# Multi-query attention block: order of the upper scores, the values and their stores

## Chip, cores and metric

The kernel runs on one core of a Trainium2 chip. A core has five engines with queues of their own: PE (TensorE, matrix products), DVE (VectorE), ACT (ScalarE), POOL (GpSimd) and SP, which here only issues DMA transfers. Each engine works through its queue in order, and they wait for each other by semaphores. The metric is the device time of one execution in microseconds (us).

## What is computed

Sixty-four batches of 128 tokens with 512 features. Each is normalized, sixteen query heads of 64 features share one key and one value head, a null key and value stand ahead of the tokens, a bias for each head is added, a causal mask (which lets each token see the null place, the tokens up to itself) and a mask of absent tokens apply, and the output projection is normalized and added to the input.

```
xn  = layernorm(x) * g_in
q   = (xn @ Wq) as 16 heads of 64, times 64**-0.5
k, v = halves of xn @ Wkv, with the null key and value ahead
sim = q k^T + bias ; causal and token masks -> -max
out = softmax(sim) v ; out = out @ Wo
y   = x + layernorm(out) * g_out
```

All is in float32.

## The kernel before

The order of the instructions is written by hand; tiles with a fixed number of buffers make the waits. Batches are in groups of four (GB = 4). A main loop runs over steps n; step n projects queries for a group ahead, computes keys and values of batch n + 6, scores of batch n + 2, exponentials of batch n + 1 and the weighted values of batch n. Steps up to 57 (P_LAST + 2, with P_LAST = 55) are step_a for even n and step_b for odd n; they form the output projection of two batches with seven half-size products (out_product). Steps 58 to 63 are last_step, which has no query projection left and forms the output projection directly (out_mm).

Scores come in two halves: a "lower" one, the queries of the first 64 tokens against 64 keys (tile lo or the first half of ps), and an "upper" one, the last 64 tokens against 128 keys (tile ps, two PSUM banks, one buffer). Rows for both lie in one SBUF tile S (s in the profile), already filled with bias and mask by POOL (bias_add, L514). The score products (L547) land in PSUM, DVE adds them into S (scores_add: L563 for the split lower home, L565 otherwise) and takes the negative row maximum (scores_max, L570); ACT takes exponentials with the row sums (exps, L579), DVE the reciprocal of the sums (rinv, L596), POOL scales (scale, L600). DVE then transposes S in 32x32 blocks into sb, which has one buffer (blocks_T, L615); in the next step PE multiplies sb with the values vr into four PSUM tiles po (values, L644), and ACT moves them with the null value added into oT (values_out, L661), from which the output projection reads.

region(n) stands at the end of each step and issues: scores of n + 2, lower and upper; the lower add and maximum; values and values_out of batch n; blocks_T of batch n + 1; the upper add of n + 2. The upper maximum follows early in the next step (max_hi). lower_home gives the lower scores two half tiles: in the early steps one in the pool ps_y (tag Y, which is also the home of the normalized output yn, L782 to L788), in steps after 57 one in ps_q (tag a, which the values use too), and always one in ps_w (tag w, two buffers, which the values use too).

Keys and values: kv_mm (L343) gives both for a batch, kv_out (L358) puts them into kvt, a tile of a whole group with one buffer. After the fourth batch of a group, at the end of the step, keys_T transposes the keys into kb (L386), stores them to memory as kd (to_tokens, three DMAs, L367) and loads them back in four copies as kT (L395); values_spread then stores the values as vd (again L367) and loads them in four copies as vr (L378). All of these DMAs are issued by SP, in order, with the batch loads (L122), residual loads (L129) and stores of results (L817).

In the last steps, last_step(n) issues the output product of batch n - 1 (out_mm), then region(n). In step 61 only half of that product is issued ahead of region, the other half in step 62, likewise there.

## Time and profile before

| | |
|---|---|
| median of 3 runs | 1093.63 us (1092.07 to 1096.82) |
| profiled execution, its own time | 1091.44 us |
| its span, first to last instruction | 1089.7 us |
| PE busy | 1059.1 us (97%) |
| PE weight loads | 885.2 us (81%) |
| DVE busy | 769.1 us (71%) |
| ACT busy | 704.3 us (65%) |
| POOL busy | 703.3 us (65%) |
| mean granted TensorE clock | 0.998 |

How to read what follows. A row of the order of time has the start, the duration, the engine, the line, the operation, output and inputs, shapes and count; in square brackets stands the idle time of the engine just before it and what ended it. A row of the waits says who waited for whom, the total in us, how often, and the longest. The chain of waits is followed back from the last instruction to whatever released it. A group row has line, engine, operation, shapes and count, then busy us and mean ns, then idle time before.

### The profile page before, as it was taken

What the parts mean: (1) busy time and instruction counts of PE and PEld (TensorE: products, weight loads), DVE (VectorE), ACT (ScalarE), POOL (GpSimd) and SP (SyncE); (2) the same over time, 40 slices, a digit from 0 to 9 for tenths busy, and PEclk for the clock granted to TensorE, in tenths of its full rate; (3) what the DMA queues carried; (4) which work ended last, traced back from release to release, by engine and by line L of the source; (5) the groups of instructions that cost most, each with busy time, mean ns of one, the idle gap of its engine ahead of it and who ended that gap; (6) DMA issues with size and microseconds to landing.
All of it is one profiled execution on the core that took longest, in us unless ns stands there. A gap on an engine that the chain in (4) does not pass through costs nothing.

```text
span 1089.7 us, 31299 instructions
## 1 busy us (share of the span) xinstructions
PE 1059.1 (97%) x12292; PEld 885.2 (81%) x12292; DVE 769.1 (71%) x1576; ACT 704.3 (65%) x2826; POOL 703.3 (65%) x520
## 2 busy tenths in 40 slices
PE   8989999999999999999999999999999999999887
PEld 7776887888888888888888888888888888888443
DVE  4767677776777777777777777777777777666772
ACT  3446676675676676676676767667667676656672
POOL 3656767576675767667576676758667576756562
PEclk9999999999999999999999999999999999999999
DMA  6413413423134331423424133341413333111211
GB/s 201 140 47 110 142 64 101 137 59 123 62 96 137 89 119 50 134 84 101 137 63 130 64 121 98 101 137 48 139 60 116 114 98 103 58 41 42 74 53 69
DMA packets 69076, 105.14 MB, mean 96 GB/s; under 512 B 9536, under 2 KB 33728, under 8 KB 67136
## 3 DMA queue, kind: packets, MB, share of 16 engines
q1 hardware_dynamic: 68112, 102.08, 30.4%
q8 instruction: 97, 1.59, 0.6%
q10 hardware_dynamic: 816, 1.05, 0.3%
q14 instruction: 51, 0.42, 0.1%
HBM read 67.45 MB, written 35.65 MB: 95 GB/s over the span
## 4 chain that ended last, share of the span: by engine, by line
PE 88%; DVE 4%; DMA 3%; ACT 2%; issue 1%; SPq 1%; POOL 0%; ACTq 0%; DVEq 0%; POOLq 0%
PE pa L476 17%; PE pyX L728 17%; PE pc L476 9%; PE pyY L728 9%; PE po L644 8%; PE pkv L343 5%; PE ps L547 5%; PE pw L476 4%; PE py L675 4%; PE pyw L728 4%; PE lo L547 3%; PE pq L425 1%; ACT s L579 1%; DVE y L788 1%; DMA biasp<-in_fside_16xSxS_dram 1%
## 5 line engine op out<-in xcount | busy, mean ns | idle before, releaser
L579 ACT ACTIVATE s<-s,nmax 128x65 f32<-128x65 f32 (+1 forms) x1024 | 373.2, 373 | 1.4 <-DVE nmax L570 1.4
L600 POOL TENSOR_TENSOR s<-s,rinv 128x512 f32<-128x512 f32 (+1 forms) x128 | 189.5, 1480 | 200.0 <-DVE rinv L596 192.7
L514 POOL TENSOR_TENSOR s<-biasp,mneg 128x1552 f32<-128x1552 f32 x64 | 207.0, 3234 | 68.5 <-DVE sb L615 66.5
L661 ACT ACTIVATE oT<-po,nv 128x256 f32<-128x256 f32 x256 | 100.7, 475 | 158.0 <-PE po L644 157.9
L579 ACT ACTIVATION_READ_ACCUMULATOR s<-s,nmax 128x1 f32 x1024 | 200.1, 195 | 0.0
L728 PE MATMUL pyX<-wT,oT 128*128 128x256 f32 x672 | 161.7, 383 | 0.0
L615 DVE STREAM_TRANSPOSE sb<-s 128x1536 f32<-128x1536 f32 x64 | 113.8, 1778 | 57.1 <-PE po L644 55.0
L728 PEld LDWEIGHTS pyX<-wT,oT 128*128 128x128 f32 x672 | 125.4, 190 | 20.7 <-issue 4.8
L476 PE MATMUL pa<-xS,wq 128*128 128x256 f32 x480 | 123.5, 380 | 1.0 <-ACT ku L487 1.0
L570 DVE TENSOR_REDUCE nmax<-s 128x8 f32<-128x520 f32 (+1 forms) x128 | 122.1, 954 | 2.4
L476 PEld LDWEIGHTS pa<-xS,wq 128*128 128x128 f32 x480 | 90.9, 190 | 14.2 <-ACT ku L487 1.8
L644 PE MATMUL po<-sb,vr 32*64 32x128 f32 (+1 forms) x4096 | 92.4, 306 | 5.8 <-DVE s L563 3.3
L644 PEld LDWEIGHTS po<-sb,vr 32*64 32x64 f32 x4096 | 71.7, 131 | 21.3 <-issue 15.8
L487 ACT COPY ku<-pa 128x256 f32<-128x256 f32 x120 | 44.7, 372 | 64.7 <-PE pa L476 59.5
L565 DVE TENSOR_TENSOR s<-ps,s 128x1024 f32<-128x1024 f32 (+1 forms) x66 | 77.3, 1171 | 2.3 <-PE ps L547 2.3
L708 POOL TENSOR_TENSOR yS<-oT 128x512 f32<-128x512 f32 x28 | 35.7, 1277 | 63.8 <-ACT oT L661 63.8
L563 DVE TENSOR_TENSOR s<-lo,s 128x256 f32<-128x256 f32 x124 | 46.7, 418 | 41.3 <-PE lo L547 41.3
L343 PEld LDWEIGHTS pkv<-wkv,xT 128*128 128x128 f32 x512 | 64.3, 191 | 14.1 <-issue 8.8
L343 PE MATMUL pkv<-wkv,xT 128*128 128x128 f32 x512 | 70.5, 281 | 5.0 <-ACT xT L304 2.5
L547 PE MATMUL ps<-kT,qT 64*64 64x128 f32 (+1 forms) x2112 | 70.0, 268 | 0.0
L291 ACT ACTIVATE x<-x,nmr,rstd 128x512 f32<-128x512 f32 x60 | 48.7, 815 | 27.9 <-DVE nmr L278 25.5
L785 DVE TENSOR_TENSOR yn<-yn,gob 128x512 f32<-128x512 f32 x56 | 39.2, 700 | 38.7 <-ACT yn L782 38.7
(99 smaller groups left out, 2076.9 us busy)
## 6 DMA issues: line engine op xcount, KB each, us to landing
x<-in_x_dram SPq DMA_DIRECT2D x64, 256.0 KB
res<-in_x_dram SPq DMA_DIRECT2D x64, 256.0 KB
out_dram<-y SPq DMA_DIRECT2D x64, 256.0 KB
xd<-xb SPq DMA_DIRECT2D x14, 1024.0 KB
xT<-xd SPq DMA_DIRECT2D x56, 256.0 KB
vr<-vd SPq DMA_DIRECT2D x64, 128.0 KB
kT<-kd SPq DMA_DIRECT2D x64, 64.0 KB
wo<-in_L_cond_Wo_dram SPq DMA_DIRECT2D x1, 2048.0 KB
```

The costliest lines, as they stand in the source:

```text
L343: nc.tensor.matmul(pkv, xT[g][:, t, kc, :], wkv[:, kc, :], start=(kc == 0), stop=(kc == KC - 1),)
L476: nc.tensor.matmul(prod[tag], w[:, kc, f * P : (f + 1) * P], t[:, :, kc, :], start=(start and kc == 0), stop=(kc == HK - 1), skip_group_ch ...
L514: nc.gpsimd.tensor_tensor(S[b], biasp, mneg[:, t].unsqueeze(1).broadcast_to([P, R8, ROW]), ALU.add,)
L547: nc.tensor.matmul(home[r][u * DH : (u + 1) * DH, f, :], qT[g][rows, f, t, hf, u], kT[g][rows, 0 : nk // Q, t, :], start=True, stop=True,)
L565: nc.vector.tensor_tensor(sv, pv, sv, ALU.add)
L570: nc.vector.tensor_reduce(nmax[b][:, hf], S[b][:, :, WITH_NULL[hf]], AX.X, ALU.max, negate=True)
L579: nc.scalar.activation(row, row, AF.Exp, bias=nmax[b][:, hf, k : k + 1], accum_out=rsum[b][:, hf, k : k + 1],)
L600: nc.gpsimd.tensor_tensor(sv, sv, rinvs.pop((b, hf)).unsqueeze(2).broadcast_to([P, R8, sv.shape[2]]), ALU.mult,)
L615: nc.vector.transpose(sb.rearrange("p j e q -> p e j q"), S[b][:, :, 1 : ROW - 1].rearrange("p e (j k) -> p e j k", k=Q),)
L644: nc.tensor.matmul(po[s][rows, to : to + n], vr[g][quad, j, t, :], sb[quad, slots, r * NF : (r + 1) * NF, :], start=(turn == 0), stop=True ...
L661: nc.scalar.activation(oT[b][:, u * NF : (u + 1) * NF, :].rearrange("p f (s q) -> p s f q", q=Q)[:, blocks], po, AF.Identity, bias=nv2,)
L728: nc.tensor.matmul(prod[key], h[:, c, :], w[:, c, :], start=(start and c == 0), stop=(c == HC - 1), skip_group_check=not start,)
```

## The change

The stores of a group's values are issued in kv_out when the group's fourth batch is in, and values_spread only loads them back. In region, the steps up to 57 (early) keep PE's order and add the upper scores ahead of the transpose. The steps after 57 compute the lower scores in the tile of the upper ones, then the values, and the upper scores behind the transpose in the order of issue. In region the values are issued for every step; it is only called from step 0 on.

```diff
+    def to_tokens(out, places):
+        for at, to, n in ((0, 0, 2), (2, 3, 1), (3, 2, 1)):
+            nc.sync.dma_start(
+                out=out[to * Q : (to + n) * Q], in_=places[at * Q : (at + n) * Q]
+            )
+
+    kvts, vds = {}, {}
-    kvts, kvds = {}, {}
 
     def kv_out(m, pkv):
...
             ALU.subtract,
         )
-
-    def to_tokens(out, places):
...
+        if t == GB - 1:
+            vds[g] = dp.tile([P, GB * DH], FP, tag="vd", name=f"vd_{g}")
+            to_tokens(vds[g], kvts[g][:, 1].rearrange("p t d -> p (t d)"))
 
     def values_spread(g):
 
-        vd = dp.tile([P, GB * DH], FP, tag="vd", name=f"vd_{g}")
-        to_tokens(vd, kvts[g][:, 1].rearrange("p t d -> p (t d)"))
+        vd = vds.pop(g)
...
     def lower_home(n):
 
-        pool, tag = (ps_q, "a") if n > P_LAST + 2 else (ps_y, "Y")
         tiles = [
-            pool.tile([P, HE], FP, tag=tag, name=f"lo0_{n}"),
+            ps_y.tile([P, HE], FP, tag="Y", name=f"lo0_{n}"),
             ps_w.tile([P, HE], FP, tag="w", name=f"lo1_{n}"),
         ]
...
     def region(n):
         nb, eb = n + 2, n + 1
+        early = n <= P_LAST + 2
         if nb < B:
-            scores(nb, 0, lower_home(n))
-            scores(nb, 1)
+            scores(nb, 0, lower_home(n) if early else None)
+            if early:
+                scores(nb, 1)
             scores_add(nb, 0)
+        values(n)
+        if nb < B:
             scores_max(nb, 0)
-        if n >= 0:
-            values(n)
-            values_out(n)
+            if early:
+                scores_add(nb, 1)
+        values_out(n)
         if 0 <= eb < B:
             blocks_T(eb)
         if nb < B:
-            scores_add(nb, 1)
+            if not early:
+                scores(nb, 1)
+                scores_add(nb, 1)
             late_max.append(nb)
```

More of the change, by code (lines that the diff above doesn't have):

```diff
@@ L363, in kv_out @@
         )
-    def to_tokens(out, places):
-        for at, to, n in ((0, 0, 2), (2, 3, 1), (3, 2, 1)):
-            nc.sync.dma_start(
-                out=out[to * Q : (to + n) * Q], in_=places[at * Q : (at + n) * Q]
-            )
+        if t == GB - 1:
+            vds[g] = dp.tile([P, GB * DH], FP, tag="vd", name=f"vd_{g}")
+            to_tokens(vds[g], kvts[g][:, 1].rearrange("p t d -> p (t d)"))
     def values_spread(g):
-        vd = dp.tile([P, GB * DH], FP, tag="vd", name=f"vd_{g}")
-        to_tokens(vd, kvts[g][:, 1].rearrange("p t d -> p (t d)"))
+        vd = vds.pop(g)
         vr[g] = hp.tile([P, NQ, GB, DH], FP, tag="vr", name=f"vr_{g}")
```

## The prediction

> **What bounds the kernel now.** I read the chain of waits first, then the busy time by stage and the waits of PE, then the order of time where PE stops.

> ```profile
> span 1089.7 us, 31299 instructions
> ...
> PE 88%; DVE 4%; DMA 3%; ACT 2%; issue 1%; SPq 1%; POOL 0%; ACTq 0%; DVEq 0%; POOLq 0%
> ```

> The span of the profiled execution is 1089.7 us, its time 1091.44 (1.74 around the span), and 88% of the chain that ends last is TensorE. An edit on another engine therefore pays only where PE stops for it.

> ```profile
> 133.00:1009.00 876.00, 869.62 (x10374) 749.41 (x10368) 638.45 (x1334) 590.73 (x2371) 584.23 (x424) 1.00 0.31 95
> 1009.00:1089.70 80.70, 67.72 (x765) 35.29 (x760) 46.49 (x79) 45.68 (x197) 39.71 (x29) 0.97 0.20 65
> ```

> Columns: stretch, its length, busy us of PE, weight loads, DVE, ACT and POOL, granted clock, DMA share, GB/s. From 133 to 1009 us (steps 4 to 57) PE stands still for 6.4 us in 876. In the last 80.7 us (steps 58 to 63 and the end) it is idle for 13.0, and there the clock is below 1. So the early steps and the late steps are two problems.

> PE's waits from 133 to 1009, and where the pair product that opens each even step starts (first, two in the middle, last; the first three from the chain, the fourth from the order of time):

> ```profile
> PE po L644 <- issue: 2.4, 2, 1.9
> PE lo L547 <- DVE y L788: 1.6, 8, 0.2
> PE pkv L343 <- issue: 1.6, 1, 1.6
> ```

> ```profile
> 133.09 1.93 PE pyX L728 x8
> ...
> 622.63 1.92 PE pyX L728 x8
> 654.68 1.92 PE pyX L728 x8
> ```

> ```profile
> 1009.01 1.99 PE L728 MATMUL pyX<-wT,oT 128*128 128x256 f32 x8
> ```

> Two undisturbed steps take 654.68 - 622.63 = 32.05 us. From 133.09 to 1009.01 lie 27 such pairs: 27 x 32.05 = 865.3, but 875.9 passed. That is more than PE's idle time, since the modelled ends of matmuls cover part of a wait. Of the excess of 10.6 us, 4.0 are "issue", waits for nothing that the profile shows, which this change has no hand in. About **6.6 us** are left that other engines cost PE in the early steps. That is the most that the early part can give there.

> **Part 1: values to memory ahead of the keys' transpose.** Nothing is added: three stores per group (L367) are issued at kv_out of the group's fourth batch instead of behind the keys' three stores and four loads.

> ```profile
> DVE kvt L358 <- DMA vd<-kvt: 7.2, 10, 1.1
> ...
> DVE sb L615 <- PE po L644: 55.0, 62, 2.9
> ```

> ```profile
> SPq L367 <- DVE kb L386: 222.4, 14, 15.9
> ...
> SPq L367 <- DVE nmr L278: 10.4, 1, 10.4
> ```

> ```profile
> 295.61 1.82 SPq L367 DMA_DIRECT2D kd<-kb  x3
> ...
> 301.79 1.67 SPq L367 DMA_DIRECT2D vd<-kvt  x3
> ```

> ```profile
> 304.72 0.29 DVE L358 TENSOR_TENSOR kvt<-pkv,nkv 128x128 f32<-128x128 f32 x1 [1.09 <-DMA vd<-kvt]
> ```

> The tile kvt has one buffer, so the next group's first kv_out cannot write before the values have been read out. In this group the keys' stores went out at 295.61, the values' at 301.79, and DVE stood 1.09 us at 304.72 for them. DVE is in order: behind that kv_out wait q_out, rinv, the statistics, the gain and the residual of the pair (L788), and the residual frees the bank into which PE writes the next lower scores: this is the row "lo <- DVE y". Moved to the fourth kv_out, the values go out nearly a step earlier and are in memory long before; the 7.2 us of DVE waits go to nothing. The queue has room: SP waits 222.4 us in 14 times for the keys' transpose, about 15.9 us each, and 10.4 once at the start; three stores take 1.67 us of it. Nothing stands behind them there but the keys' own stores, and everything that follows the spreading (batch loads, at the start the late weights) leaves SP earlier by those 1.67 us and a landing. Cost 0; if that room were gone, 1.67 us of SP per group, with the keys not needed until the step after.

> **Part 2: upper scores added ahead of the block transpose, early steps.** PE's and ACT's order stays; on DVE two instructions change places.

> ```profile
> 620.22 1.06 PE L547 MATMUL ps<-kT,qT 64*64 64x128 f32 x32
> ...
> 621.33 0.69 DVE L570 TENSOR_REDUCE nmax<-s 128x8 f32<-128x520 f32 x1
> ...
> 622.82 1.78 DVE L615 STREAM_TRANSPOSE sb<-s 128x1536 f32<-128x1536 f32 x1 [0.79 <-PE po L644]
> ...
> 624.52 1.19 DVE L565 TENSOR_TENSOR s<-ps,s 128x1024 f32<-128x1024 f32 x1
> 624.74 3.24 POOL L514 TENSOR_TENSOR s<-biasp,mneg 128x1552 f32<-128x1552 f32 x1 [0.68 <-DVE sb L615]
> ...
> 628.45 1.27 POOL L458 TENSOR_TENSOR xS<-xT 128x512 f32<-128x512 f32 x1
> ...
> 630.46 1.03 PE L476 MATMUL pa<-xS,wq 128*128 128x256 f32 x4
> ```

> The lower maximum ends at 622.02; the transpose waits 0.79 us for the values product (55.0 us over 62 steps). The upper scores are done at 620.22 + 1.06 = 621.28, so their add can start at 621.95 (an instruction that waits for nothing starts about 0.08 before its predecessor's end: 622.82 + 1.78 against 624.52) and takes 1.19 - 0.08 = 1.11 to the next start: the transpose starts at 623.05 instead of 622.82, **0.23 later**, and what follows on DVE comes 1.11 - 0.23 = **0.9 earlier**. Late next is the bias add on POOL, which waits for the transpose in the even steps: 0.23 later, and behind it in POOL's queue the power for the norm, the token sums and the scaling. The token sum ends at 629.72 and PE uses it at 630.46: slack 0.74, of which 0.23 go. With that cover gone it would be 0.23 per step.

> Both parts push the same way: DVE reaches q_out, gain and residual 0.9 us sooner and without the wait for the store. The pair 622.63 to 654.68, where the values happened to be stored in time, ran at 32.05 already; I take that for all. Bounds: 0 (something else holds the residual) to 6.6; taken **6.0**, since the undisturbed pair shows no next wait.

> **Part 3: the last steps.** For steps 58 to 61 (62 and 63 have no scores left) PE's order becomes lower scores, values, upper scores; the lower scores use the tile of the upper ones, with one add of 128x512 in place of two of 128x256.

> ```profile
> 1019.27 0.69 PE L547 MATMUL lo<-kT,qT 64*64 64x64 f32 x32
> 1019.79 1.06 PE L547 MATMUL ps<-kT,qT 64*64 64x128 f32 x32
> 1021.40 1.41 PE L644 MATMUL po<-sb,vr 32*64 32x256 f32 x64 [0.55 <-DVE s L563]
> 1023.63 7.13 PE L675 MATMUL py<-wo,oT 128*128 128x512 f32 x16 [0.82 <-ACT oT L661]
> ...
> 1034.74 7.13 PE L675 MATMUL py<-wo,oT 128*128 128x512 f32 x16 [0.82 <-ACT oT L661]
> ...
> 1053.51 1.88 PE L644 MATMUL po<-sb,vr 32*64 32x256 f32 x64 [2.49 <-DVE s L563]
> 1055.31 8.25 PE L675 MATMUL py<-wo,oT 128*128 128x512 f32 x16
> ```

> Now the values wait for DVE to read the lower scores (their bank is reused) and the output product waits 0.82 for ACT to empty the values. Step 58 to 59 takes 1034.74 - 1023.63 = 11.11. Behind the change the upper scores (1.0 us) fill the 0.82, and the values wait for no add: PE needs 7.13 + 0.52 (start of the lower to start of the upper scores) + 1.41 + 1.06 = 10.1 a step; whole durations are a little long, which leaves room for the changes of kind. First output product: 1019.27 + 0.52 + 1.41 + 1.06 = 1022.3 against 1023.63, 1.3 gained; after two more steps 3 are.

> Then the softmax loop decides. Rows of step 59 (order of time of DVE and of POOL) and the last one of step 61:

> ```profile
> 1025.91 1.23 DVE L570 TENSOR_REDUCE nmax<-s 128x8 f32<-128x1032 f32 x1
> ...
> 1030.40 0.20 DVE L596 RECIPROCAL rinv<-rsum 128x8 f32<-128x8 f32 x1 [1.53 <-ACT s L579]
> ...
> 1052.52 0.20 DVE L596 RECIPROCAL rinv<-rsum 128x8 f32<-128x8 f32 x1 [1.53 <-ACT s L579]
> ```

> ```profile
> 1030.68 1.91 POOL L600 TENSOR_TENSOR s<-s,rinv 128x1024 f32<-128x1024 f32 x1 [1.11 <-DVE rinv L596]
> ```

> Maximum to reciprocal 4.49 (ACT's upper exponentials in it), 0.28 to the scaling, 1.91, transpose 1.78 - 0.08, upper add 1.19: 9.57 us round. PE's 10.1 is just longer, but it starts 1.3 ahead. Two rounds from 1030.40 bring the reciprocal of step 61 to about 1049.5 instead of 1052.52: 3.0 sooner. In step 61 the output product has only half its length, so PE comes early and waits there for the lower add (now ahead of the upper scores, not of the values): done about 1049.5 + 0.69 = 1050.2, upper scores to 1051.4, output product 1051.4 against 1055.31, **3.9**.

> ```profile
> L565 DVE TENSOR_TENSOR s<-ps,s 128x512 f32<-128x512 f32 x2 | 1.4, 691 | 0.8 <-PE ps L547 0.8
> ```

> ```profile
> 1055.00:1057.00 2.00, 2.00 (x18) 0.84 (x3) 1.43 (x1) 1.61 (x5) 0.93 (x1) 0.50 0.11 40
> ```

> The single lower add (0.69) costs what the two do. But the new wait of PE, from the values' end (1022.3 + 2 x 10.1 for the half product, 3.6, 0.52 and 1.41: 1048.0) to 1050.3, is 2.3 us, about as long as the old one of 2.49, after which the granted clock was 0.50: the values took 1.88 instead of 1.41 and the 16 products 8.25 instead of 7.13, 1.6 us in all. I expect that again, slightly dearer because upper scores and products both fall into it. Bounds of the tail: 1.3 (only the first step's) to 5.0 (no drop: the 1.1 of the products on top); taken **3.5**.

> [...]

> **Sum.** 1091.44 - 6.0 - 3.5 = 1081.9 against this execution. The median of the runs shown is 1093.63, 2.2 above it, which gives 1084.1; I say **1083**.

> **Rivals.**
> - *Only the tail pays* (the early excess stays: something else, such as ACT's second norm, holds the residual). For it: the waits of PE for L788 are 0.2 each, little beside DVE's 1.1. Against: the undisturbed pair. 1092.5 (the middle of the two bases) - 3.5 = 1089. Chance 0.14.
> - *Only the early steps pay*: the wait moves from the values to the upper scores in each late step and the clock falls oftener. For it: step 61 does just this. Against: in steps 58 to 60 DVE reads the lower scores while PE runs the values. 1092.5 - 6 = 1086.5. Chance 0.14.
> - *Slower*: the transpose's 0.23 reaches PE at every step. It decides once the path transpose, bias add, power and token sum has less slack than 0.23 at PE; then 54 early steps cost 54 x 0.23 = 12.4, the store's gain is lost on the same path, and the tail gives 3.5: 1092.5 + 12.4 - 3.5 = 1101. Against: slack 0.74, and DVE's 0.9. Chance 0.07.
> - *Nothing*: the values are stored in time anyway and the tail's end is set elsewhere: 1092.5. The 13.0 us of idle PE speak against it. Chance 0.03.

> **Numbers.** The forecast has 0.62. Half a per cent, what a measurement of this kernel can tell from no change, is 5.5 us: faster means below 1088.2, slower above 1099.1. The forecast nearly whole, most of "only early" and a third of "only tail" lie below: 0.74; slower 0.07; the rest 0.19. All best bounds (6.6 + 5.0, and up to 2 between executions) give 1078; upwards 1090 takes in "only the tail".

> **What would show it.** The wait of kvt for vd is gone; the upper add stands ahead of the transpose and the latter's wait for the values is nearly gone; from the first to the last pair product 870 us or less instead of 875.9, "issue" included; PE's wait of the values for DVE gone and one of 2 to 3 us ahead of the last upper scores, with the clock at 0.5 behind it; the last products starting 9 to 10 us sooner. Wrong if the early excess stays at 6, if POOL's token sum makes PE wait, or if a late step still takes 11 us.

## The result, and the profile after

The changed kernel takes **1077.51 us**, the median of four runs (1076.90 to 1079.76), against 1092.85 for four runs of the kernel before beside it: a ratio of 0.9857, 95% interval 0.9828 to 0.9886. Run again on another occasion it took 1080.22 (ratio 0.9884, 0.9869 to 0.9898). Its profiled execution took 1079.76 us, 11.7 less than the one before.

The page of the changed kernel (span, and the chain of waits by engine):

```profile
span 1078.0 us, 31342 instructions
...
PE 91%; DVE 2%; POOL 2%; DMA 2%; ACT 2%; issue 1%; ACTq 0%; SPq 0%; DVEq 0%; POOLq 0%
```

The two stretches, cut at the first and the last pair product as before (stretch, length, busy us of PE, weight loads, DVE, ACT, POOL, granted clock, DMA share, GB/s):

```profile
133.10:1001.20 868.10, 866.11 (x10368) 748.92 (x10368) 641.22 (x1335) 590.55 (x2371) 583.79 (x424) 1.00 0.30 96
1001.20:1078.00 76.80, 67.97 (x765) 35.09 (x760) 45.66 (x75) 45.52 (x197) 39.68 (x29) 0.97 0.20 67
```

The early stretch went from 875.92 to 868.10 us, **7.8** less, and the last one from 80.69 to 76.80, **3.9** less. Both profiles start the stretch at 133.1, so the 11.7 are these two.

PE's waits that matter, in the changed kernel (who for whom, total, times, longest):

```profile
PE po L645 <- issue: 2.0, 2, 1.2
PE ps L548 <- DVE s L566: 1.9, 1, 1.9
```

The wait of the lower scores for the residual ("lo <- DVE y") has no row any more, nor has DVE's wait for the store of the values. Three pair products from the chain of waits, and the last from PE's order of time:

```profile
133.10 1.92 PE pyX L729 x8
...
229.26 1.93 PE pyX L729 x8
262.34 1.93 PE pyX L729 x8
```

```profile
1001.20 1.99 PE L729 MATMUL pyX<-wT,oT 128*128 128x256 f32 x8
```

The first three pairs take (229.26 - 133.10) / 3 = 32.05 each. The fourth takes 33.08, one of two longer ones; both hold an issue wait. Against the floor of 27 x 32.05 = 865.35, 2.75 us are left of the 10.6 before: 2.0 of issue waits and 0.75 of all the rest. By the pairs, the two with an issue wait hold 2.6 of it, so most of the 0.75 is what such a wait costs beyond its length.

DVE's order of time in step 57, the last early one:

```profile
999.97 0.69 DVE L571 TENSOR_REDUCE nmax<-s 128x8 f32<-128x520 f32 x1
1000.59 1.22 DVE L566 TENSOR_TENSOR s<-ps,s 128x1024 f32<-128x1024 f32 x1
1001.72 1.77 DVE L616 STREAM_TRANSPOSE sb<-s 128x1536 f32<-128x1536 f32 x1
```

The upper add stands ahead of the transpose, and the transpose no longer waits for the values (no bracket).

PE's order of time in the last steps:

```profile
1014.48 7.13 PE L676 MATMUL py<-wo,oT 128*128 128x512 f32 x16
...
1024.55 7.13 PE L676 MATMUL py<-wo,oT 128*128 128x512 f32 x16
...
1038.88 1.42 PE L645 MATMUL po<-sb,vr 32*64 32x256 f32 x64
1042.23 1.26 PE L548 MATMUL ps<-kT,qT 64*64 64x128 f32 x32 [1.94 <-DVE s L566]
1043.43 8.62 PE L676 MATMUL py<-wo,oT 128*128 128x512 f32 x16
```

A late step takes 1024.55 - 1014.48 = 10.07 us instead of 11.11, and no wait stands in it. In step 61 PE waits 1.94 us, now ahead of the upper scores. The clock behind it:

```profile
1044.00:1046.00 2.00, 2.00 (x3) 0.67 (x2) 2.00 (x2) 2.00 (x13) 0.83 (x1) 0.50 0.16 58
```

It is halved again, and the 16 products take 8.62 instead of 7.13.

### The profile page after: what moved, and what is told of

The parts are those of the page before. It is cut to its first block, busy times and chain, and to the rows that moved or that the text cites. A ratio compares the mean times of both kernels' runs of the same rounds, so it can differ in the third digit from the quotient of the medians.

```text
span 1078.0 us, 31342 instructions
## 1 busy us (share of the span) xinstructions
PE 1055.6 (98%) x12292; PEld 884.2 (82%) x12292; DVE 771.3 (72%) x1572; ACT 703.9 (65%) x2826; POOL 702.9 (65%) x520
## 3 DMA queue, kind: packets, MB, share of 16 engines
q8 instruction: 97, 1.59, 0.6%
## 4 chain that ended last, share of the span: by engine, by line
PE 91%; DVE 2%; POOL 2%; DMA 2%; ACT 2%; issue 1%; ACTq 0%; SPq 0%; DVEq 0%; POOLq 0%
PE pa L478 19%; PE pyX L729 18%; PE pc L478 10%; PE pyY L729 9%; PE po L645 7%; PE pkv L343 6%; PE ps L548 5%; PE pw L478 5%; PE pyw L729 4%; PE lo L548 3%; PE py L676 3%; PE pq L427 1%; DMA x<-in_x_dram 1%; ACT s L580 1%; POOL s L516 1%
## 5 line engine op out<-in xcount | busy, mean ns | idle before, releaser
L566 DVE TENSOR_TENSOR s<-ps,s 128x1024 f32<-128x1024 f32 (+1 forms) x70 | 81.7, 1167 | 2.8 <-PE ps L548 2.7
L564 DVE TENSOR_TENSOR s<-lo,s 128x256 f32<-128x256 f32 x116 | 43.8, 420 | 47.8 <-PE lo L548 47.7
L548 PE MATMUL ps<-kT,qT 64*64 64x128 f32 (+1 forms) x2240 | 72.2, 266 | 1.9 <-DVE s L566 1.9
L343 PE MATMUL pkv<-wkv,xT 128*128 128x128 f32 x512 | 70.4, 281 | 3.5 <-ACT xT L304 2.7
L343 PEld LDWEIGHTS pkv<-wkv,xT 128*128 128x128 f32 x512 | 64.3, 191 | 11.5 <-issue 4.6
L499 DVE TENSOR_TENSOR qT<-pc,ku 128x256 f32<-128x256 f32 x120 | 49.4, 412 | 25.2 <-ACT ku L489 19.0
```

Source lines behind the costliest of these rows:

```text
L343: nc.tensor.matmul(pkv, xT[g][:, t, kc, :], wkv[:, kc, :], start=(kc == 0), stop=(kc == KC - 1),)
L548: nc.tensor.matmul(home[r][u * DH : (u + 1) * DH, f, :], qT[g][rows, f, t, hf, u], kT[g][rows, 0 : nk // Q, t, :], start=True, stop=True,)
L566: nc.vector.tensor_tensor(sv, pv, sv, ALU.add)
```

## The experiments

There are 7.8 us to explain in the early steps, of which 1.8 came in addition to the 6.0 of the sum, and 3.9 in the last ones. The theory to begin with: the early gain is DVE's, freed from its wait for the store, and the tail is a part of its own. Rivals: the moved upper add does it, or something else falls away with the stores.

### e1: the stores moved, nothing else

```diff
+        if t == GB - 1:
+            vds[g] = dp.tile([P, GB * DH], FP, tag="vd", name=f"vd_{g}")
+            to_tokens(vds[g], kvts[g][:, 1].rearrange("p t d -> p (t d)"))
...
-        vd = dp.tile([P, GB * DH], FP, tag="vd", name=f"vd_{g}")
-        to_tokens(vd, kvts[g][:, 1].rearrange("p t d -> p (t d)"))
+        vd = vds.pop(g)
```

> The kernel before with the values' stores moved to the fourth kv_out and nothing else. Theory (the store's wait made the early excess of 6.6 us, and more of it in the executions without a profile, whose times scatter from 1091.8 to 1096.8): no wait of kvt for vd, pairs of steps at 32.05 us apart from issue waits, profile 6 us shorter, times 6 to 11 us shorter and closer together. Rival (the DVE order made it): under 2 us.

Measured: 1081.52 us against 1092.86, ratio 0.9901 (0.9867 to 0.9936). The early stretch is 868.57, DVE waits for no store, and all of its pairs but the two with issue waits (2.4 us in all) stand at 32.05 to 32.12. So the stores alone give nearly the whole early part. The gain of 11.3 us is a little more than the 6 to 11 expected: in the profile 7.4 are the early stretch, 1.9 an earlier first pair product (131.21) and 1.9 the tail.

The tail, which keeps its old order here, is 78.82 instead of 80.69. PE's order of time in it, and the stretch behind the wait:

```profile
1044.21 1.41 PE L646 MATMUL po<-sb,vr 32*64 32x256 f32 x64 [2.49 <-DVE s L565]
```

```profile
1044.00:1046.00 2.00, 1.79 (x65) 1.49 (x66) 0.96 (x3) 0.39 (x2) 2.00 (x2) 1.00 0.00 0
```

The wait is the 2.49 us of the kernel before, to the hundredth, but the clock stays at 1.00 behind it. This is where the tail's 1.9 us come from; no part of the edit reaches there, so they are luck (the last section says of what kind).

### e2: the upper add moved, nothing else

```diff
             values(n)
+            if nb < B and early:
+                scores_add(nb, 1)
             values_out(n)
...
-            scores_add(nb, 1)
+            if not early:
+                scores_add(nb, 1)
```

> The kernel before with the upper scores added ahead of the block transpose in the steps up to 57 and nothing else. Theory (kvt still waits for the values' store, which leaves SP at the same time as before): DVE's 0.9 us go into longer waits for vd, 16 of them and together about 15 us more, and the time is within 2 us of before. Rival (DVE's order makes the gain): 6 us shorter or more.

Measured: 1091.97 us, ratio 0.9991 (0.9970 to 1.0013), early stretch 877.34. DVE's and PE's waits:

```profile
DVE kvt L358 <- DMA vd<-kvt: 22.6, 14, 1.8
...
DVE sb L615 <- PE po L644: 6.3, 6, 1.4
...
PE lo L547 <- DVE y L788: 2.7, 13, 0.2
```

The transpose's wait for the values falls from 55.0 to 6.3 us, so DVE is some 0.9 us sooner, and it spends this at the store: 22.6 us there, from 7.2. In order behind it, the residual comes no earlier. Alone the move gives nothing that can be measured; what it gives with the stores out of the way is not told apart from the 868.57 of e1 and 868.10 of the whole.

### e3: the last steps changed, nothing else

```diff
-            scores(nb, 0, lower_home(n))
-            scores(nb, 1)
+            scores(nb, 0, lower_home(n) if early else None)
+            if early:
+                scores(nb, 1)
...
         if nb < B:
+            if not early:
+                scores(nb, 1)
             scores_add(nb, 1)
```

> The kernel before with the last steps' order alone (lower scores in the upper ones' tile, values, upper scores). Theory: 3.9 us shorter as the profile of the changed kernel shows between the last pair product and the end, steps of 10.1 us, a wait of PE of 1.9 us ahead of the last upper scores and the clock at 0.5 behind it. Rival (the late steps owe part of it to the early ones): under 2 us.

Measured: 1089.40 us, ratio 0.9960 (0.9937 to 0.9984), tail 77.07, early stretch 877.79: 3.5 us less in the medians, 3.9 expected. The tail stands by itself. Within their intervals (0.002 to 0.0035 to either side) the three parts add up: 0.0099 + 0.0009 + 0.0040 = 0.0148, against 0.0143 for the whole and 0.0116 when it was run again.

### e4 and e5: the wait removed in another way, and the order of SP's queue

To tell DVE's wait from what else the earlier stores do, e4 keeps the stores late and gives kvt a second buffer. (To make room for it, the small tiles nmax, rsum and rinv have three buffers instead of four.)

```diff
-            kvts[g] = hp.tile([P, 2, GB, DH], FP, tag="kv", name=f"kvt_{g}", bufs=1)
+            kvts[g] = hp.tile([P, 2, GB, DH], FP, tag="kv", name=f"kvt_{g}", bufs=2)
```

> The kernel before with two buffers for kvt (three instead of four for nmax, rsum and rinv to make room); the stores stay where they are. Theory (it is the reuse of kvt, and not the place of the stores in SP's queue, that cost time): no wait of kvt for vd and the same gain as with the early stores, within 1.5 us. Rival (the gain comes from SP's shorter queue, loads leaving earlier): within 2 us of before.

Measured: only 1088.99 us, ratio 0.9971 (0.9949 to 0.9992), early stretch 878.04, although DVE waits for no store any more. The 3.9 us are neither the gain of the early stores, which was expected, nor the rival's 2 or less. From the chain of waits, three pair products, then PE's waits:

```profile
229.95 1.92 PE pyX L728 x8
245.10 2.75 issue
268.00 1.92 PE pyX L728 x8
300.06 1.92 PE pyX L728 x8
```

```profile
PE po L644 <- issue: 5.2, 2, 2.7
...
PE pkv L343 <- issue: 1.9, 1, 1.9
```

The undisturbed pair takes 32.06, the one with the issue wait 38.05. There are three such waits, 7.1 us in all, and their price is more than their length: every pair without one takes 32.05 or 32.06, so the three pairs with one hold all of the 12.7 us above the floor. DVE's part is thus gone in e4 as well; what eats it up are the issue waits. The stretches around the longest one:

```profile
245.00:247.00 2.00, 0.10 (x7) 0.00 (x0) 0.00 (x0) 1.20 (x3) 0.00 (x0) 1.00 0.88 229
247.00:249.00 2.00, 1.15 (x5) 0.85 (x5) 0.67 (x1) 0.74 (x4) 0.19 (x1) 0.57 0.36 123
249.00:251.00 2.00, 2.00 (x9) 1.82 (x9) 2.00 (x2) 0.72 (x5) 1.92 (x2) 0.50 0.13 49
```

PE stands, the DMA engines are at 0.88, and behind it the granted clock is 0.50. Beside the wait that "nothing in the profile shows" stands a row after all, in the table of DMA queues. It is there on the page of the kernel before (queue, packets, MB, share of 16 engines):

```profile
q8 instruction: 97, 1.59, 0.6%
```

Instructions have a queue among those of the DMA engines, with 97 packets of 1.59 MB / 97 = 16.4 kB and 0.6% of the time of the 16 engines. The same table of e4, for 0.2 us from 245.4:

```profile
q1 hardware_dynamic: 38, 0.07, 88.0%
q8 instruction: 1, 0.02, 28.8%
```

One instruction packet starts there, in the midst of data at 88%, and PE goes on at 247.85. In all thirteen profiles (before, after and the eleven runs) I set the issue waits of PE over 0.2 us behind 100 us beside the starts of these packets: there are 22, and each ends 2.3 to 3.9 us after a packet starts, or 1.2 to 1.6 us after it has landed. All 22 stand at the same three places of PE's program: after 3485, 5007 or 6529 of its 24,584 matmuls and weight loads, in every profile that has one there. From this I read that PE stands until its instructions have come; no row says it. At the second place the start of the packet tells the wait: where it starts after 4751 to 4836 of them, PE then waits 0 to 0.8 us; where it starts after 4904 to 5007, 1.2 to 2.75. That the packets come late because data stands ahead of them is what e5 tries. It has the same two buffers, but the loads of coming batches and the mask leave SP ahead of the values' stores and loads, which go out behind them:

```diff
             load_mask(g + 1)
+        if q and f == 0 and n > 0:
+            values_spread(g - 1)
...
-                values_spread(g)
+                if g == NG - 1:
+                    values_spread(g)
```

> As e4_kvt_two (two buffers for kvt, values' stores late), but the next batch loads and the mask load leave SP ahead of the values' stores and loads (which move to the start of the next step), the last group excepted. Theory (behind the keys, SP's queue holds the batch loads back by the stores' 1.7 us and their landing; they then crowd the transfers together at the place where PE's next instructions are due, and PE's issue waits grow): issue waits of PE fall from the 7.1 us of e4 to 3 or less, and the time to within 2 us of e1_stores_early (1081.5). Rival (issue waits are chance and have nothing to do with the order): issue waits of 4 to 8, time within 2 us of e4 (1089.0).

Measured: 1078.99 us, ratio 0.9875 (0.9861 to 0.9890), early stretch 866.91, issue waits of 0.6 us in all: 10 us less than e4 for an order of DMA issues. SP's order of time in e4, then in e5:

```profile
235.94 1.75 SPq L378 DMA_DIRECT2D vr<-vd  x4
237.73 1.23 SPq L122 DMA_DIRECT2D x<-in_x_dram  x2
```

```profile
231.00 1.15 SPq L122 DMA_DIRECT2D x<-in_x_dram  x2
232.72 1.64 SPq L367 DMA_DIRECT2D vd<-kvt  x3
...
240.82 2.36 SPq L378 DMA_DIRECT2D vr<-vd  x4
```

The pair product of e5 starts at 227.88, so the batch loads leave 3.1 us after it, 7.8 in e4. The DMA queues of e5 for 0.2 us from 240.8 have one row:

```profile
q8 instruction: 1, 0.02, 32.3%
```

The packet starts 240.8 - 227.88 = 12.9 us into the pair, against 245.4 - 229.95 = 15.5 in e4, with no data packet starting beside it, and no wait over 0.2 us follows it. The 2.6 us by which it comes later in e4 are close to the 2.75 that PE waits there. The kernels differ in the place of the batch loads and of the values' transfers at once, so which of the two matters more is not settled; nor is why only three of the fourteen groups have such waits.

The change moves the same loads, by less. Before, pair product and batch loads (the chain, and SP's order of time), then SP's row of the changed kernel, whose pair product starts at 229.26:

```profile
231.72 1.92 PE pyX L728 x8
```

```profile
239.25 1.24 SPq L122 DMA_DIRECT2D x<-in_x_dram  x2
```

```profile
234.74 1.28 SPq L122 DMA_DIRECT2D x<-in_x_dram  x2
```

7.5 us after the pair product before, 5.5 after the change. Over all profiles:

| order on SP | profiles | issue waits of PE, us |
|---|---|---|
| values' stores late, batch loads behind them | before, e2, e3, e4 | 4.0, 3.4, 3.2, 7.1 |
| stores early, batch loads behind the values' loads | after, e8 (after again), e1, e6, e7, e11 | 2.0, 0, 2.4, 1.5, 0.2, 1.7 |
| batch loads first | e5, e9, e10 | 0.6, 0, 0.5 |

The first order overlaps with neither of the others. The second and the third do overlap: in the second the waits scatter from 0 to 2.4 between profiles, in the third from 0 to 0.6.

Most packets leave no such wait behind: of the 97 in the kernel before, three stand ahead of an issue wait of PE over 0.2 us, 4.0 us in all; in e4 three waits take 7.1 us. The row does not name the engine; that the late packets are PE's own is inferred from PE's standing, always at the same three places.

### e6: the transpose later still

The slower rival rests on the transpose's delay reaching PE. In the changed kernel the lower maximum is taken twice, ahead of the transpose, in the early steps; the result is the same.

```diff
-        if hf == 0:
+        if hf == 0 and b not in nmax:
...
+                scores_max(nb, 0)
```

> The changed kernel with the lower maximum taken a second time between the upper add and the block transpose in the steps up to 57 (0.69 us more DVE work there, the transpose 0.6 us later again). Theory (slack 0.74 behind the transpose, 0.23 used): 0 to 10 us longer, less than a third of 58 x 0.6. Rival (a later transpose reaches PE in every step): 58 x 0.6 = 35 us longer.

Measured: 1083.34 us, ratio 0.9914 (0.9895 to 0.9934), 3.1 above the changed kernel beside it (e8). Pair products from the chain of waits, then a wait of PE:

```profile
620.53 1.92 PE pyX L729 x8
652.89 1.92 PE pyX L729 x8
684.95 1.93 PE pyX L729 x8
```

```profile
PE pa L478 <- POOL xS L460: 0.3, 1, 0.3
```

A further 0.6 us on the transpose, 54 times, would cost some 32 us without slack. One pair in two takes 32.36 or so instead of 32.06. So the slack that the prediction read from the token sum (0.74) is real, and of nearly that size: 0.23 + 0.6 just begins to show.

### e7 and e11: half a product into PE's last wait

PE's one wait in the last steps is in step 61. Here the second half of the output product of batch 60 is issued between values and upper scores of that step, and in step 58 the copy of the last pair product stands ahead of four exponentials.

```diff
+        if n == B - 3:
+            out_mm(n - 1, HC)
...
-        if n == B - 2:
-            out_mm(n - 2, HC)
+            out_part(p4 + 1, 0, "X")
...
-            out_part(p4 + 1, 0, "X")
```

> The changed kernel with two more edits in the last steps: in step 61 the second half of the output product of batch 60 is issued between the values and the upper scores, where PE waits 1.9 us, and in step 58 the copy of the last pair product is issued ahead of four exponentials, where PE waits 1.2 us. Theory: the wait of 1.9 us and the half clock behind it go (3.5 us in the profile), and 1.2 from step 58: 4 to 5 us shorter than the changed kernel. Rival (the softmax loop of 9.65 us sets these steps): under 1.5 us shorter.

> The kernel of e7 once more, on the same chip as e9 and e10: 1071 to 1075, tail 73. If the gain of e7 was the chip's, it will lie with e9 at 1077 to 1080 instead.

Measured: 1073.37 us, ratio 0.9824 (0.9808 to 0.9841), tail 73.05; again, 1074.08, ratio 0.9839 (0.9797 to 0.9882), tail 73.1. It is faster than both kernels. The tail is 3.75 us shorter than the 76.80 of the changed kernel, a little under the 4 to 5 expected; of the 6.9 us to e8 beside it, 3.0 are an earlier first pair product (131.79 for 134.81), which the edit does not touch. PE's order of time in e7:

```profile
1035.21 1.42 PE L645 MATMUL po<-sb,vr 32*64 32x256 f32 x64
1036.56 3.70 PE L676 MATMUL py<-wo,oT 128*128 128x512 f32 x8
1040.19 1.10 PE L548 MATMUL ps<-kT,qT 64*64 64x128 f32 x32
1041.23 3.70 PE L676 MATMUL py<-wo,oT 128*128 128x512 f32 x8
```

No bracket, and eight products take 3.70 us each time, as they do at a clock of 1.00 (1034.62 in the changed kernel): with the wait, the halved clock behind it goes too. The wait for the copy in step 58 falls from 1.21 to 0.46 us.

### e8, e9, e10: the changed kernel again, and with the batch loads first

e8 is the changed kernel itself, beside e5 to e7. e9 has the edit of e5 made to the changed kernel, where it puts the batch loads ahead of the values' loads alone (the stores are early already); e10 is e9 with the edit of e7.

> The changed kernel once more, for the spread of its times and a second profile. Theory (its profiled execution, 1079.76, had 2.0 us of issue waits, a start 1.8 us later than the best seen and the clock drop of step 61): times between 1074 and 1081, and a profile in which these three terms explain the difference to the first one to within 1 us. Rival: the profile differs in the pairs of steps or the late steps themselves.

> The changed kernel, with the batch loads and the load of the next mask issued on SP ahead of the four loads of the values (vr) instead of behind them. Theory (SP's order decides how much PE stands in issue waits): the loads leave some 2 us sooner, the issue waits of PE stay under 1 us in all, the early stretch is 865 to 867, and the median is 1077 to 1079, at or below the best profiles of the changed kernel. Rival (the three stores were all that mattered, issue waits are chance): the early stretch scatters between 866 and 869 as in the two profiles of the changed kernel. Second rival: the values' loads, now later, make PE wait for vr: a new wait of the values product for the DMA of vr.

> The same order of loads together with the late steps in which half an output product fills PE's wait of step 61. Theory: the two add up, early stretch 865 to 867, tail 73, 1071 to 1074, PE's issue waits under 1 us. Rival: the order of loads has nothing left to give beside the changed kernel; then it lies within 1 us of the same kernel without it (e11).

Measured: e8 1080.22 us (1078.92 to 1081.24), at the upper end of what was expected. Its profile has no issue wait, an early stretch of 865.90, and a first pair product at 134.81 instead of 133.10. Its clock falls in the same place, to 0.50. Start and early stretch together, 1.7 more and 2.2 less, explain the 0.4 between the two profiled executions.

e9 took 1077.72 us (ratio 0.9869, 0.9835 to 0.9903), early stretch 865.73, no issue wait; the values' later loads make no wait on PE. e10 took 1075.40 (0.9848, 0.9813 to 0.9883), e11 beside it 1074.08. So the order of the loads has little left to give once the stores are early: e9 lies among the runs of the changed kernel, and e10 above the 1071 to 1074 expected and not below e11. In the profiles a little shows: the early stretch is 866.24 in e10 and 867.82 in e11, but e10's first pair product comes at 134.23 and that of e11 at 131.68, which hides it.

## Why the prediction was right, and where not

**The stores.** Right. The early steps cost 6.6 us beyond the floor and the issue waits before, 0.75 after: 5.9 gained where 6.0 were taken. This counts an issue wait at its length, and it costs more. By the pairs, 3.6 of the 10.6 before lie in pairs without an issue wait and are gone; 6.9 lie in the three pairs with one. Alone, such waits make a pair 0.15 to 0.4 longer than they are (changed kernel, e1, and the 1.9 us in e4), so an estimate gives 4.4 to 5.2 of the 6.9 to them and the rest to DVE: 5.3 to 6.1 for DVE's part in all. e1 shows that the stores do it, e2 that the moved add alone does not.

**The issue waits.** This is the step that failed: "Of the excess of 10.6 us, 4.0 are "issue", waits for nothing that the profile shows, which this change has no hand in." The change does have a hand in them, by a move that the prediction itself lists: "everything that follows the spreading (batch loads, at the start the late weights) leaves SP earlier by those 1.67 us and a landing. Cost 0". The loads do leave 2.0 us earlier, and the issue waits fall from 4.0 to 2.0 in one profile of the changed kernel and to 0 in the other. They stand in the same places of PE's program in all profiles and are longer, at the second of them, where the instruction packet comes later (0 to 0.8 us against 1.2 to 2.75). e4 and e5, alike but for the order on SP, differ by 6.5 us of issue waits and 10 us of time. With this, the early part is 7.8 to 10 instead of 6.0, and its best bound was 10.6, not 6.6. The row of the instruction queue was on the page before, and was not read.

**The transpose 0.23 later.** Right: no wait for it on PE, and e6 measures the slack.

**The last steps.** The mechanism was right and the size, 3.5, was 0.4 short. From the last pair product to the first output product it gained 1.3, as said: 1023.63 - 1009.01 = 14.62, now 1014.48 - 1001.20 = 13.28. The step takes 10.07 for 10.1. The softmax loop, from DVE's order of time in the changed kernel:

```profile
1022.12 0.20 DVE L597 RECIPROCAL rinv<-rsum 128x8 f32<-128x8 f32 x1 [1.53 <-ACT s L580]
...
1031.77 0.20 DVE L597 RECIPROCAL rinv<-rsum 128x8 f32<-128x8 f32 x1 [1.53 <-ACT s L580]
...
1041.41 0.20 DVE L597 RECIPROCAL rinv<-rsum 128x8 f32<-128x8 f32 x1 [1.53 <-ACT s L580]
```

It takes 9.65 a round for 9.57. The new wait is 1.94 for 2.3, with the clock at 0.50 behind it, as forecast. The last whole output product comes 1055.31 - 1009.01 = 46.30 after the last pair product before and 1043.43 - 1001.20 = 42.23 now, 4.1 sooner for 3.9. The clock's part costs 0.4 more than before (8.62 for 8.25), and the tail as a whole gains 3.9. This compares two tails with the halved clock. Against the old tails that kept theirs (78.8 to 78.9 in e1, e2 and e4) the new order's 76.8 is 2.0 less, so part of the size is luck. Of the signs that the prediction named, the new wait is just below its 2 to 3 us, and the last products start 11.9 us sooner (1043.43 for 1055.31) for 9 to 10; the difference is the issue waits again.

**The sum.** 1081.9 was worked out against the profiled execution, which took 1079.76. Of the 2.1 between them, 1.8 are the issue waits (less 0.15 that DVE did not give) and 0.4 the tail. The median of 1077.51 lies 2.2 below that execution, while the median of the kernel before lay 1.4 above its own; the prediction had moved its sum upwards for this, by 1.1 to 1083. Against 1083 the first comparison lies 5.5 us low and e8 2.8. In the profiles three things differ between executions of nearly the same code: the first pair product starts anywhere from 131.2 to 135.3, the issue waits go from 0 to 2.4, and the old tail is 78.8 to 78.9 or 80.4 to 80.7 by the clock. The four profiles with the late starts (e2, e6, e8 and e10, at 134.2 and later) have the clock at 0.50 for 3.4 us near 24 us, the other nine, at 133.2 or before, have not; half of 3.4 is the 1.7 us by which e8's start is later. The runs of the first comparison have a mean clock of 0.998, those of e8 0.996 or 0.997, so one such fall more is an estimate for some 1.7 of the 2.7 us between their medians. The rest stays open.

**The rivals.** "Only the tail" and "only the early steps" fell with e1 and e3, which show each part by itself; "slower" fell with e6.

## What to carry to other kernels

When PE waits for "issue", look at the table of DMA queues for the instruction queue in that stretch: here instructions shared the DMA engines with data (in e4 a packet of 16.4 kB started amid data at 88.0%), and a burst of loads that left two to five microseconds later went with issue waits of PE that were 2 to 6.5 us longer. So the order in which one queue issues its DMAs can have a price of its own, 10 us between e4 and e5, even where PE's waits have no data transfer among them, as in e4; ask of each moved transfer what it now stands beside. And a wait that is removed on an in-order engine is worth something only if the next wait on that engine isn't the same one in another place, as the moved add alone showed: of DVE's waits 55.0 us became 6.3, 7.2 became 22.6, and the time stayed (ratio 0.9991).

## What was not expected of the hardware

```profile
1050.77:1054.18 3.41, 0.92 (x45) 0.70 (x35) 1.75 (x5) 2.33 (x11) 2.29 (x3) 1.00 0.00 0
```

```profile
1039.51:1042.93 3.42, 2.21 (x66) 1.33 (x64) 2.12 (x6) 3.26 (x17) 2.88 (x3) 1.00 0.02 5
1042.93:1046.34 3.41, 2.13 (x66) 1.68 (x67) 2.07 (x5) 1.61 (x6) 2.83 (x2) 1.00 0.00 0
```

In before one stretch holds the whole wait, 3.41 - 0.92 = 2.49 us idle, and the clock falls behind it. In e1 an edge cuts the wait into 1.21 and 1.28, and the clock stays. Over the thirteen profiles, behind 100 us and up to the last products, it fell behind nine stretches in which PE was idle for 1.92 to 2.49 us, and behind none with 1.90 or less; one with 2.00, near the end of e3, is the exception. So in these traces, with that one exception, 1.92 us or more of idle time in one stretch went with a fall, 1.94 in the changed kernel. How a wait lies to the edges is luck here: the same 2.49 us lie whole in a stretch in before and cut in two in e1. This is read from the profiles alone; no run was made to test it.

The issue waits can cost more than their length: the 2.75 us in e4 made its pair 6.0 us longer, since the clock stayed at 0.50 for 6.8 us behind it, half of which is 3.4. There, eight products of keys and values took 2.00 us in the chain of waits, and 1.09 at 283.17, where no wait stands ahead.
